# Moving one elementwise multiply of a gated attention layer from VectorE to GpSimd

## The chip, the core and the metric

The kernel runs on one NeuronCore of a Trainium2 chip. The core has five engines that run side by side, each through its own list of instructions, strictly in order: TensorE (PE) for matrix products, VectorE (DVE), ScalarE (ACT) and GpSimd (POOL) for elementwise work, and SyncE (SP), which here only starts memory transfers. An instruction that needs another engine's output waits for it, and everything behind it on its engine waits too. GpSimd in this kernel works on SBUF alone; PSUM, where TensorE writes, is read by VectorE and ScalarE.

The metric is the device time of one execution in microseconds, as a median over runs. It was 1340.9 us before the change (three runs, 1340.47 to 1341.65).

## The reference

One transformer layer on x of shape (4, 512, 512), all in fp32: a linear attention with 16 heads (key size 64, 64 memory slots, value size 128), a gate and a norm on its output, a layernorm, a mixture of 8 low-rank maps, and a second layernorm. What the change touches is the end of the attention:

```python
o = jnp.transpose(_chunk_abc(q, k, v, s), (0, 2, 1, 3))
g = (hidden_states @ Wg).reshape(b, t, H, DV)
o = o * jax.lax.rsqrt(jnp.mean(jnp.square(o), axis=-1, keepdims=True) + EPS) * g_norm_weight
o = o * (g * jax.nn.sigmoid(g))
return o.reshape(b, t, VALUE_DIM) @ Wo
```

The attention before it (okT is the query times hk) first sums keys into memory slots with a decay, takes a softmax over the slots, and then sums values with these weights:

```python
hk = hk * g_t[:, :, None, :] + k_t[..., None] * p_t[:, :, None, :]
pvT = jax.nn.softmax(okT, axis=-1)
hv = hv * g_t[..., None] + p_t[..., None] * v_t[:, :, None, :]
```

## The kernel before

The work is cut into 4 batch rows by 8 pairs of heads, 32 pairs in all, each over 512 time steps. Matrix products are made exact enough by splitting every fp32 operand into a rounded high part and the rest (names ending in h and l), and multiplying high by high, high by low and low by high. So nearly every value that TensorE reads is cast once (on ScalarE, mostly) and subtracted once (on VectorE or GpSimd). Weights are split once, kept in DRAM, and fetched again from there for every batch row by SP.

One pair goes through these kinds of step, each named by a letter:

- `s`, `k`, `q`, `g`, `v`: projections (decay, key, query, two gates, value), 12 matmuls of 512 columns each (value: of 256).
- `e`, `u`, `i`, `t`: transposes and states carried from one half of the time steps to the other.
- `c`: key scores (tiles `pa`), which ScalarE casts to `at`, VectorE subtracts and adds, and GpSimd cuts to the causal half (`causal`, an affine select). `x`: sums over them into `po_k`, which become `okc` (ScalarE copy `tk`, VectorE add), multiplied by `rc` on GpSimd.
- `o` (`soft`): the softmax, on VectorE, ScalarE and GpSimd. It turns `okc` over, takes maxima `mx`, subtracts (`pr`, GpSimd), exponentiates, sums `ss`, multiplies (`pr`, GpSimd), turns back, and ends in `wst`, the weights that TensorE needs next.
- `d`: value scores from `wst` and `est`; `y`: their sums into `po_v`. From `po_v` come the squares `sq`, their split `sqs`, and `t`, the output times its gate.
- `n` (`norm`, lines 972 to 1001): see below, twice for each pair, once for each head. `w` (`combine`): the output projection into `po_y`, four blocks of six matmuls that read `oh` and `ol`; VectorE adds each block to `y`.
- Letters `l`, `m`, `h`, `r`, `j`, `p`: loading and transposing x, and the second half of the layer for each batch row (`m`, `h` for the first three rows, `r`, `j` for the last). `b` and `f` start weight transfers on SP's queue, the first time and again.

The function `norm` is one matmul (`pt_ms`, the mean of squares over 128 channels) and five instructions after it, each on the engine that its `@on` names: "a" ScalarE, "d" VectorE, "p" GpSimd, "s" SP. First the logarithm and the exponential with factor -0.5 make the reciprocal norm `rstd` on ScalarE. Then VectorE multiplies `t` by it in place. Then ScalarE casts the product to `oh`, and GpSimd subtracts to get `ol`.

The order of the work is written out ahead of time, by a generator, in the string `PLAN` (lines 83 to 193). A letter alone issues the next step of that kind, that is its matmuls or its transfer. A mark and a letter issue the next instruction that a step of that kind still has for one engine: `^` ScalarE, `.` VectorE, `,` GpSimd, `;` SP; a number between them skips so many of them. So the string fixes the order on all five engines at once. Four more strings, `SLOTS`, say which of the 7 weight buffers (`wt`), 6 raw weight buffers (`wraw`), 7 work buffers (`tmp`, where `t`, `rstd`, `sq`, `cum`, `sg`, `okc` and others live) and 4 PSUM banks (`pa`) each new tile takes. A tile may be written when the one before it in its buffer has been read for the last time.

All instructions are recorded through one helper, so the profile shows line 56 for nearly all; tiles are told apart by their names.

Of the kernel before, what the change touches and what calls it, by code (L numbers as in the profile page):

```python
# [18 lines left out]
def tile_abc_attention_ffn(  # L19
# [22 lines left out]
    class InOrder:  # L42
# [41 lines left out]
        lpoooooooommoooooooooooooooooooooooorrrr,p,pbbbblbbl^l.ll^l.ll^l,b.l^l,b.ls,b;bb,1b^b,b.b^bq,b;bb.s  # L84
        ;1b.b^sb,b;bb.sek^q;b,sb.q^s,b^see.s^ke,s;b^kb^e.suuk^u^b,b.k,1b.e,b.ui.b^1k^i^i,b;bb.i.i;bb^i,ic^c
        ^c.c.1c^c;b,b.cb^k.c.cu,c^cs.k^b;p,c.c,b.c.b,c;bxb.cxx^b.s;b,cxbx.bx^sxxx.s,se;bxgb^s,s^x^s.x.sxx^ge
        ug.s^x^g.x^u,x^g.u^b.ge^g.oq^b.b^g.o;b^gb.b^o.g;bb.o^q.pv,o^b.q.b^oev^e.o;bb.e^oi^v.ov^i,o.v^i.i.i.o
        ^it,i^t.ov^t.t^o.t.o^bd^v.b^b.v;b^db.b^dg^d.d;b^d.1db.d.d,d.d,d.1d.dy^g.d,d^b,dy^g.by^g;b^yyb.g^yv
        ^1y.y^y.y.1yc,y.1y^c^c.y,y^cv.c^c.1c.yv^v.c.c,c.c,c.1cnxv.c^n.c,c.v^n,cx^b.nxxx^vx.bxxx^nx.vx;bx^xg
        ,nb^x.x^b.x.b,x;bsb^b.o.b.o;bb^o.s^s.ov,o^b.b,s^oeeee;bv.o^eb,s^o.et^v.o^t,o.v^t^g.tk.t^g.o^g.s.o^s  # L90
        .g^o^s.od^k.s^k^b.s^d.k^dq.d^d^d.1d.d.d,d.d,d.1d.du.du,d^qy.b^u,dy^b.q;byb^y.u.b^yy;b.yi^ybs.y^y^i,y
        .1y^i.1y.y.iv.i^b.s^i.b,i^sc;b.s,sb^c^c.c^sk.1c,s^c.c^s.c.c^c,c.s,c.cv.s^k,c^k.c^b.kxe^bxex.c^vux.b
        ,cxexx.vx^x;bnxb.b^n,yxxxt.x^n;bb.y^xv^t.n^t.x^nuq.t^u,x.t.u,n.o.oew^q^o.qw^e.o.w,o.ew^o.w.og^o.w.o
        ,o.op^gwb.o^p^g.pv^o.w;p^g.o^b.gd^v.b^b.v^d;b^db.dg^d.1d^d.d^b.d,d.d,d.1d.d.d,di.b^gy,d^i^g.by;bb^i
        ^gy.i;b^y.iy.gb^i^y,ink^1y.y^y.y^n.1y,y^n.1y.yc^1k.n^c^n.c^ks.c,nl^c.k^c.c^c,c.1c.c.c,c.cp,c.sxvb^p
        .c^b.p,c^sl.b;p^b,st.s;b^lbx,sv^t^t.l^su.tx^vx.tnx.b^sx,ynx^n.vx;bexbv.y^n.s^x.nxxxv.s^n.x^x,n.xp^vu
        vb,x^p.v^u.p^bv.o^b;p^b.u.o^be.bq^v^o.b;bb.v^b;b.ob^b.b,ow.b;b^qb^oeg.q;bb.o.w^o.b^b.o;bewb.b^e,o.b
        ;b^bbg^n.o^g;bb.e^n^g.o.n^gw^o.w^g.gw^g.o^n.w^g.wd,n.g^d^d.d^d.1ds^d.d.d,d.d,d.1d.d.d,d.bi,d^iy.s^i
        ;bby.i^s.it^i.s,s^1yy^t^t.ty^s.t,i^yg,s^s.y^y.s^y.y.s,y.1yc^g.y^c^g.yk^c.c^g.1c^c.c^c.g,c.c.c,cx.1cp
        ^k.cx^kb.c,c^p.kuex^b,cx.pxx^bee.bx;px^xxx.bv^b;bb.x^b;b^b.bbxxn^b.bv;b,y^xb.b;b^nbg^n.y;bb^v.x.n,x  # L100
        .v^n.bq^g,n^g.o;bb^g.o.g^ow^q.o,o.qw.w^o.onu.we^ow^u.o^e.uv,o^n.w.e^nn.ov^1n.n^1n.op^v.nwb^o.v^p.o^n
        .p^n,n.wd;p^b^d.b,n^dk^d.d;b^d.1db^b.d.d,d^b.d^b,d.1d.di.d^1k,dy.b^i^i,dy.i;b.i^ib.by^y,i.by;b^ybs.y
        ;b^yb.y^y.1y,y.1y.y,yc.s^c.y^s.c^kg.s,s^c^c^c.k^s,s.c.c^s.1cq^g.s,c^g.c^g.s,c.c.cp,c^q.gepb^px.cebx
        ^px.q,cxx^bx.pxex^xnx.p;px^bxux.x^nt.b^xl^n.b;bgb^t.x^t;p^l.n,x^b;b.t.t^b.lb^b.bw^g.o^b;bb^g.bw.o^b
        ;bb^g.wu^on.bw.g^u;bb.o.w,ov.u.w^ov.b^b.o;bb.b^ow.b;b^vb.o^ng;b.v,ob^b.w^n,n.o^n.b^bs.o^g;bb.n^g.b^o
        ^n.o;bb^ge,nw.s^e.g^s.e^b.s.wd^d^d,s^s.d^d,s.1dg^s.d.d^d.s,d.d.s,d.di.d^g,dy.b^i^gy.d;b^i,d^g.iyb.i
        ^i.gy^y,i^yv^1y.y^y.y.1yc,y.1y^c^c.y,y^cq.c^c.1c.y.c.c,c.c,cp.1c^qv.cb^p.c,c.q^b,c.p^bxxx.bx^v;pexx
        ^bx.bxxe^xx.vxx;b^bl;b.xn^xbee.b^lbw.x^n;bb.l^e,xfk^n.w.n.o.el.o^kfg.b^k^o.k;bb^l.o,o.lv^o^b.o.bu^ou
        t;b^u.ovb^t.u^t,o^g.t.t^gi.ow^v.o^g.v^i^ow.g^i.o^nf.i,n^b.i.w^i.wd^d^d,i.d^d^d.1ds.d.d,d.d,d.1d.d.d
        ,d.b,dy^b.s;byb.b^st^1y;b.s,sy^t^ty.t^s.t,sk^y^s.y^y.s^y.y.s,y^1kf.1yc^c.y^c.y^kg^c.c^c.k.c.c,c.1c.c  # L110
        v.c^gf,c.c^g,c.ce,ce^gxxxn.gxx^nx,yxxex^x.yxn^nxx.xev^x.n^e.x^nqf.e^v,xf.v,n.o.on^qwf^o.qu.ov.w,o^ow
        .o^ow.w.ou,oq.w^u^n.u.o^2n^n.o^1n.n^ow.nf.o^nf.wd^nf,n^d^d.d,n^d.1dv^d.d.d,d.d,di.1d^vy.d^i.d,d^i.v
        ,dy.i.i^iy,i^y^yy.ys^y.y^y,y.1y.1y.y,yc^b.s^c.y^s.c^ck.s,s^q^c^c.q^s,s.c.c^s.1cg^k.s,c^k^b.c.s,c.c.c
        xt,c^gf.k^txe^g.cxx.b,cxv^t^g.t;b.t.bux.gx;bx^xxnx.xx^nexv^x^n.xef.ne^vv,xf^e.v.ew.o.ow.w^o.ouv.w,o
        ^u.u^og^v.o.v^o.o,ov^gf^g.oi^g.ow^i.g^i^o.i.iw.o^i,i.w^nf.wdf,n^d^d.d^d.1ds^d.d.d,d.d,d.1d.d.d,dy,d
        .sfy^st^1y.s,s^ty^t.tv^s.t,s^y^s.yy^b.sk^v.y^y.s^y,y.v^b.y.yc^1kf.y^c.b^c^k.cg;b^c.1c^c.k.c.c,c.c,c
        .1cv^gf.c.c,c^g.b,cx^gxux;bee.gnxx^nu,yxxxe^ux.y^nxxx.uv^x.n^x.x^ne.xg^v,n^e.v.e,xw.o^gf.o^gv^o.w^g
        .mw.g.o,oi.w^iq^i.m^o.i.o^m^m.m^o.mwf.i^q.o^i.q,om.wm^2m,i.og^2m.m.o^o.3m.ow^gf.3m^gf^g.wdf.g^d^d.m
        ^dv.d^d.d^m.d^m,dg^b.mf^v.m.d.d,d.1d.d.d,dm.v^gfy,d^m.bm^gy.m;b^mn^g.my^y.gy^yk^n.y^y.y^n,y^y.n.y^nf
        .yc^1k,n^c.y^c^ks^c.k^c.c.1c.c.c,c.cnqf,c.1cb.c,y.c.s,c.y,c^s.sxx,s^qexexxt.q^sx,sg^n^s^n.s^t.n^t^x  # L120
        .su^nxefx.th^g.t,n.x^g^g.gxx^hxw^h^b,hex.w^ev^x.b.e;bnhb.x^n,x^n.n.on^hw.o^hf^1n,hw.w^o^1n.nuv^u.w^b
        .o.u,ow.b^v^nfg.v^o;b,nb^n.w.o,n^oh.o^gf,o^g^g.o.gw^hf.o^hw^o.w^b.oi.bm^i^i.w;bw^m,h.i.i^i,i.wd^d^d
        .d^d.1dh^d.d.d,d.d,d.1d.d.d,dy,d^hfm^hy.m,hm^yy.m^yy.ym.y^yk^y.m,y.1y.y.ym^1k,yf.mc.y^c^c^k.cs^m.1c
        ^c.k^c.m.c.c,c.cnqf,c.1c.c.c,c.s,c^s.s,sxx^qxfmv.q^m^s,s.m^nxxv^s^n.s.nmf^vxfee.sx^mumx.v^xxh^1m.xxx
        .mufx^ut^x.ue^mh.x^t.m^t,x.t.t.ogf.m.o^m^o.m.om,of^om.m.om^o.m.ow.m,o^nf.oe^gvf,n^e.w^g.ov^g.e^o.gn
        ^vm.o^n.vf^n.mdf.n^d^d.d^n.1dh^d.d,n^d.d.d.1d,d.d.d,dm,dyf^m,dt.m^ti^my^t.m^iy^i^y.t.ty^y.i.i^ig.y^y
        ,i.y^y.1y,y.1y.y,yc^gf^g.y^c^gs.c^c.g^c.c^c.c,c.1c.cx.cm,cf.ch,c.s.c^s,c.s,sxxfxx^sexx,s^mxk^s.m^x.s
        ^m.x.sn.m^kxfxxv^k^n.k^nux.nee^xm.x,xn.mmm^1n.1m^1n.oeg^e.n.o.m^o.eu.omf^u,o.m.u^ow.2m^m^m.ov.m^o.m
        ;m.w;mmmmmf.o^vf.1m,o^gf.v^gwf.o^g.mg.o.g^o.w.ow.m^gf^gw^m.w^g^mf.g^nf^n.wd,n.m^d^d,n^dq.d^d;m.1d.d
        .d,d.d,d.1d.dy.d,d^qf.mi,d.q^iy;m^i.iy.i^y^iy^y,is^1y.y^y.y.1y,y.1yl.y,yc.s^c.y^s.cf^ck,s.s^c^c,s.c  # L130
        ^s.c.1c^svf.c,c^k.s^k,c.cv.s,c.cn.k^vxxex.c^nux.vx,cex^nxxxx^xx.next^x.x^te.xu^tq^e.t,x.t^u.e.u.o.ov
        ^qf^o.qi.o,o^iw^i.i.i^i^o,iw.w.ow^o.w.ow.w,o^nf.onvf,n^n.w^n.osf^v.nf^o.v^n.o,nd.sf^s^d.s,s^dg^d^d.d
        ^s.1d,s.d^s.d.d,d.sv^gf,d^g.d.sl,d^gy.d^l.gv.d.l,dy^vy.v^y^yy.yv^y.y^y,y.1yw.1y.y,y.wc.y^c^c.c^ck.1c
        ^c.c.c,c.c,c.1c.c.c,cxl^kf,cxx^kn^l.kxxux^nx.lxex^xxex^nx.xt^x.ne^ten^t.xq^e.t,x.t.e.o.ow^qf^o.quv.o
        ^u.w,o.ugf^of^v.o.v^o^1n.ow,o^gf^1n.o^gg.n^g.o.g^o.ww.o^gf^gf^n.wdf^n,n^g^d.gg,n^d.d^d^d.1d.d.d,d.d
        ,d.1dl.d^gf.dy,d^ll,d^g.li^ly^g.ly^i.g^i^yy.i^y.is^i.y^y,i.y^y.1y,y.1yw.yf,y.s.yv^s.w,s.s,sc^c^s.ck
        ^c.c^s,c.c^c.s^c.c.s,c.cev^kf.1c^k.c.c,c.kxx,c^vxxxen.vex^nnxxx^xv^n.x^1n.nx^1nxxt^x.n^tuu.xw^t^u.t
        ,x.t.uv.w.owf.o^vf^o.vw.w.o^nf,oeq.w^nf,n^e^o.e.o,n^ogf^q.o,o.q.ow^gf.o^gv^o.w^g.o.gd^d^d.d^d.1ds^d
        .d.d,d.d,d.1d.d.d,dy,d.sfv^s.s,si^vy^i.v^sy,s^i^s.iy.i^i.s^yk,i^y.s^1y.y^y.y.1y,yc^1kf.1y.y^c,y^c.c
        ^kq.1c^c.y^c.k.c.c,c.c,cv.1c^qf.c.c,c.qx,cxnxx^nxexxx^nuxx^xxe.neut^u.x^tx.ug^t^x.t.t.x,xw^gf.o^g.ow  # L140
        ^g.w^o.gv.o.w,osf^of^v.o.v^o.owf,o^nf.ovf,n.w.oev^e.s^o.e^sg.o^v.s.v^s^sdf^g.s^d.s^g,s.dg^d^g.d,s.d
        ^d.g^d,d.d.d,d.1di^gf.dv.d^i,d^g,d^i^g.iy.i^i.gy,iy^y^yy.yv^y.y^y,y.1yfc^vf.1y^c.y^c.v^ck^c.c.1c.c.c
        ,c.c,c.1cn.c^kvf.c,c^k^n,y.kn,c^n.yexxx^1nxux.nx^1nv^x.n^n.xxe^v,nt^t.vxex^tx.txx.tg^x.x,xuw.o^gf^u
        .o^g.uw^o.w^g.mv.g.o.w,ov.m^owf^m.of^v^m.v^onq.m^1n.m.o^1n.w,o.m.om^qfem^2m.og^e.n^o.q^2m.o.3mw.e^gf
        .3m^gf^n.wdf^n,n.m^g^d.gs,n^m^d.d^m.1d^d^d.m.m.d.d,dv.df,d.1d.d.dv,d.s,d^si.s,st^i^i^ty.i^t.i^s.ty,s
        .t^i^sy^y.s,iy^y.sk^v.y^y.v^y.y.1y,yc.1y^1kf.y^c,y^c.c^kv.1c^c.y^c.kv.c.c,c.c,c.1cqf^vf.c.c,c.v,cxu
        ^qufxnm^u.q^nxx.um^mxx^n.mnxx^mex.nx^xexx.meg^x.x^1n.x^1n,x.nh^gf.o^g.o^g^o.gw^1hf.o,oeh.w^o^e.o.e^o
# [47 lines left out]
    def f(t):  # L195
# [8 lines left out]
            04152041520415364201543620136541362054120536  # L204
        """,
        "wraw": """
            0123450132450132450132450132450132450132450132450132450132450132450132450132450132450132514032514032
            5140325140325140325140404032
        """,
        "tmp": """  # L210
# [1175 lines left out]
```

## Time and profile before

| | |
|---|---|
| median of 3 runs | 1340.9 us |
| the profiled execution | 1339.01 us |
| its span, first to last instruction | 1337.3 us |
| granted TensorE clock | 0.998 |
| instructions | 24043 |
| bytes moved by DMA | 212.36 MB, mean 159 GB/s |

The profile comes from one execution. Busy times are those of the intervals in which an engine had an instruction at work. PE is matmuls and PEld the loading of their stationary operand, which overlap. In rows of the form "line engine operation out<-in shapes xcount | busy us, mean ns | idle before us", the last part is the time that the engine stood idle just before these instructions, and who ended it. In the table of stretches, each engine has its busy microseconds and, in brackets, its number of instructions, and the last three columns are the granted clock, the busy share of the 16 DMA engines, and GB/s. In rows of waits, the three numbers are microseconds in total, times, and the longest. In rows of the timeline, the first two numbers are start and duration in microseconds, and square brackets hold the idle time before and its releaser.

### The profile page before, as it was taken

What the parts mean: (1) busy time and instruction counts of PE and PEld (TensorE: products, weight loads), DVE (VectorE), ACT (ScalarE), POOL (GpSimd) and SP (SyncE); (2) the same over time, 40 slices, a digit from 0 to 9 for tenths busy, and PEclk for the clock granted to TensorE, in tenths of its full rate; (3) what the DMA queues carried; (4) which work ended last, traced back from release to release, by engine and by line L of the source; (5) the groups of instructions that cost most, each with busy time, mean ns of one, the idle gap of its engine ahead of it and who ended that gap; (6) DMA issues with size and microseconds to landing.
All of it is one profiled execution on the core that took longest, in us unless ns stands there. A gap on an engine that the chain in (4) does not pass through costs nothing.

```text
span 1337.3 us, 24043 instructions
## 1 busy us (share of the span) xinstructions
PE 1317.9 (99%) x8706; PEld 1139.0 (85%) x8706; DVE 1084.5 (81%) x2075; ACT 847.2 (63%) x1858; POOL 553.5 (41%) x623
## 2 busy tenths in 40 slices
PE   9999999999999999999999999999999999999997
PEld 7878888888888888888888888888888888888885
DVE  5888999988788778877779678878778887877855
ACT  4767787766676556666566655666666666666632
POOL 8344444444434343534343533334433344453310
PEclk9999999999999999999999999999999999999999
DMA  9555767763444346433344433544444343344452
GB/s 323 181 166 174 260 197 243 251 209 119 156 143 151 127 142 205 162 130 135 98 146 139 170 111 126 188 143 135 150 142 136 101 158 127 117 136 142 143 173 95
DMA packets 94007, 212.36 MB, mean 159 GB/s; under 512 B 12992, under 2 KB 43712, under 8 KB 93888
## 3 DMA queue, kind: packets, MB, share of 16 engines
q1 hardware_dynamic: 93360, 210.56, 46.9%
q8 instruction: 69, 1.13, 0.3%
q14 instruction: 50, 0.41, 0.1%
q10 hardware_dynamic: 528, 0.26, 0.1%
HBM read 162.55 MB, written 48.23 MB: 158 GB/s over the span
## 4 chain that ended last, share of the span: by engine, by line
PE 87%; DVE 7%; ACT 3%; POOL 1%; issue 1%; DMA 0%; SPq 0%; POOLq 0%; ACTq 0%; DVEq 0%
PE po_y L56 12%; PE ps_g L56 12%; PE ps_v L56 12%; PE po_v L56 7%; PE ps_s L56 6%; PE ps_k L56 6%; PE ps_q L56 6%; PE pa L56 5%; PE po_k L56 4%; PE ps_h L56 3%; PE po_f L56 3%; PE ps_vx L56 3%; PE pt_s L56 3%; PE pt_ms L56 1%; DVE at L56 1%
## 5 line engine op out<-in xcount | busy, mean ns | idle before, releaser
L56 POOL TENSOR_SCALAR_AFFINE_SELECT at<-at 128x512 fp32r<-128x512 f32 x256 | 170.8, 689 | 137.2 <-DVE at L56 123.3
L56 PE MATMUL po_y<-wt,oh 128*128 128x512 f32 x512 | 176.2, 396 | 0.1
L56 DVE TENSOR_TENSOR at<-pa,at 128x384 fp32r<-128x384 f32 x256 | 131.5, 549 | 7.4 <-ACT at L56 6.7
L56 POOL TENSOR_TENSOR ol<-t,oh 128x512 fp32r<-128x512 f32 x64 | 85.7, 1347 | 113.4 <-ACT oh L56 112.9
L56 ACT CAST at<-pa 128x384 fp32r<-128x384 f32 x256 | 107.5, 492 | 29.9 <-PE pa L56 28.2
L56 PEld LDWEIGHTS po_y<-wt,oh 128*128 128x128 f32 x512 | 96.3, 188 | 20.2 <-DVE okc L56 0.3
L56 PE MATMUL po_y<-wt,ol 128*128 128x512 f32 x256 | 100.2, 391 | 0.2 <-POOL ol L56 0.2
L56 DVE TENSOR_TENSOR y<-y,po_y 128x512 f32<-128x512 f32 x128 | 86.8, 680 | 11.6 <-PE po_y L56 10.7
L56 POOL TENSOR_SCALAR sqs<-sq 64x512 fp32r<-64x512 f32 x64 | 50.0, 781 | 95.1 <-DVE sq L56 84.0
L56 PE MATMUL po_v<-at,vh 128*128 128x256 f32 (+1 forms) x512 | 87.4, 278 | 0.0
L56 POOL TENSOR_TENSOR okc<-okc,rc 128x512 f32<-128x512 f32 x32 | 43.8, 1370 | 98.6 <-DVE okc L56 98.6
L56 PE MATMUL po_k<-at,ee 128*128 128x256 f32 (+3 forms) x512 | 82.9, 287 | 0.9 <-POOL at L56 0.8
L56 ACT ACTIVATE sq<-po_v 64x512 f32<-64x512 f32 x128 | 75.1, 591 | 9.5 <-PE po_v L56 7.5
L56 PEld LDWEIGHTS po_v<-at,vh 128*128 128x128 f32 x512 | 77.9, 190 | 0.9
L56 ACT ACTIVATE sg<-ps_g 128x512 f32<-128x512 f32 x64 | 38.2, 597 | 60.7 <-PE ps_g L56 55.7
L56 PEld LDWEIGHTS po_k<-at,ee 128*128 128x128 f32 (+1 forms) x512 | 69.0, 163 | 5.8 <-POOL at L56 2.1
L56 POOL TENSOR_TENSOR pr<-pr,mx 128x512 f32<-128x512 f32 x32 | 34.0, 1062 | 90.3 <-DVE mx L56 89.9
L56 POOL TENSOR_TENSOR pr<-pr,ss 128x512 f32<-128x512 f32 x32 | 33.9, 1059 | 88.5 <-DVE ss L56 62.4
L56 PE MATMUL po_v<-at,vl 128*128 128x256 f32 (+1 forms) x256 | 69.9, 273 | 0.3 <-POOL at L56 0.3
L56 DVE TENSOR_TENSOR at<-at,pa 128x128 fp32r<-128x128 f32 x256 | 62.8, 279 | 0.4
L56 DVE TENSOR_TENSOR t<-po_v,gate 128x512 f32<-128x512 f32 x64 | 44.1, 689 | 20.9 <-ACT sq L56 18.0
L56 POOL TENSOR_SCALAR est<-et 128x512 fp32r<-128x512 f32 x32 | 39.0, 1218 | 52.3 <-PE pa L56 23.7
(303 smaller groups left out, 3873.5 us busy)
## 6 DMA issues: line engine op xcount, KB each, us to landing
wt<-kept_v SPq DMA_DIRECT2D x48, 512.0 KB, 3.7
wt<-kept_g SPq DMA_DIRECT2D x48, 512.0 KB, 3.4
wt<-kept_o SPq DMA_DIRECT2D x48, 512.0 KB, 3.7
wt<-kept_s SPq DMA_DIRECT2D x24, 512.0 KB, 4.0
wt<-kept_k SPq DMA_DIRECT2D x24, 512.0 KB, 3.8
wt<-kept_q SPq DMA_DIRECT2D x24, 512.0 KB, 3.7
kept_g<-wt SPq DMA_DIRECT2D x16, 512.0 KB, 5.5
kept_v<-wt SPq DMA_DIRECT2D x16, 512.0 KB, 4.1
```

The costliest lines, as they stand in the source:

```text
L56: ins = fn(*args, **kwargs)
```

## The change

In `norm`, the multiply of `t` by `rstd` is issued to GpSimd in place of VectorE. Everything else that is computed, and with which instruction on which engine, stays. `PLAN` and the four strings of `SLOTS` were generated again for the kernel with this instruction on GpSimd, so the order of steps and the turns of the buffers differ in most lines.

```diff
-        @on("d")
-        def _():
-            DVE.tensor_mul(t1, t1, j.pop("rstd"))
+        @on("p")
+        def _():
+            POOL.tensor_mul(t1, t1, j.pop("rstd"))
```

The beginning of `PLAN`, where the projections of query and key change places, and its end:

```diff
-        lpoooooooommoooooooooooooooooooooooorrrr,p,pbbbblbbl^l.ll^l.ll^l,b.l^l,b.ls,b;bb,1b^b,b.b^bq,b;bb.s
-        ;1b.b^sb,b;bb.sek^q;b,sb.q^s,b^see.s^ke,s;b^kb^e.suuk^u^b,b.k,1b.e,b.ui.b^1k^i^i,b;bb.i.i;bb^i,ic^c
...
+        lpoooooooommoooooooooooooooooooooooorrrr,p,pbbbblbbl^l.ll^l.ll^l,b.l^l,b.ls,b;bb,1b^b,b.b^bk,b;bb.s
+        ;1b.b^sb,b;bb.s^k;b,s^kbuue.ke^ueq^s,b.u^s.s,s;bb.sek^q,b^e.q^b,1b.e,b.bi^1k^i,b;b^ib.i.i;bb^i,ic^c
...
-        .m^yy.yh.y^y^y,y.1y.1y.y,ywf.m.y^mnw.w^n.m^nn.nw^1n.w^nfm^n.wf,n.nm.m^n,nm.mw.mw.w.rw.w^r^r.rw.r.wfh
...
+        .mfy^my^y.m^yy.yh.y^y^y,y.1y.1y.y,ywf.m.y^mnw.w^n.m^nn.ww,n^1n^nfm^n.wf,nm,n.m^nm,n.mw.mw.w.rw.w^r^r
```

The buffers' turns begin to differ in the same way, for the weights (`wt`) for instance:

```diff
-            0123456013245061324506245013415034156203415062341503462150346210534104162041530416256302564162543016
...
+            0123456012345601234560345612415624150362415603241562410536241056324564510645326451031260314510342651
```

## The prediction

> **What bounds the kernel now.** I read the page first: busy time by engine, then the chain that ended last.
>
> ```profile
> PE 1317.9 (99%) x8706; PEld 1139.0 (85%) x8706; DVE 1084.5 (81%) x2075; ACT 847.2 (63%) x1858; POOL 553.5 (41%) x623
> ...
> PE 87%; DVE 7%; ACT 3%; POOL 1%; issue 1%; DMA 0%; SPq 0%; POOLq 0%; ACTq 0%; DVEq 0%
> ```
>
> TensorE (PE) is busy for all but 19 us of the span. Next I asked for the busy time in five stretches, to see where those 19 us lie.
>
> ```profile
> 0.00:50.00 50.00, 45.72 (x264) 38.62 (x266) 34.79 (x60) 29.50 (x63) 32.13 (x44) 1.00 0.88 290
> 50.00:100.00 50.00, 47.02 (x347) 40.95 (x344) 42.79 (x84) 33.47 (x73) 21.92 (x25) 1.00 0.48 158
> 100.00:300.00 200.00, 198.79 (x1361) 172.42 (x1360) 184.59 (x346) 151.91 (x327) 90.41 (x97) 1.00 0.66 221
> 300.00:1300.00 1000.00, 998.41 (x6620) 865.15 (x6619) 801.76 (x1545) 623.16 (x1374) 407.78 (x458) 1.00 0.42 142
> 1300.00:1337.30 37.30, 27.99 (x125) 21.86 (x123) 20.60 (x43) 9.15 (x22) 1.29 (x1) 0.92 0.31 109
> ```
>
> The first column pair after the stretch is PE. It idles 4.3 us in the first 50, 3.0 in the next, 1.2 in the next 200, 1.6 in the thousand after, 9.3 in the last 37. The changed multiply runs from 64.7 to 1267.3 us, so of all idle time only 3.0 + 1.2 + 1.6 = 5.8 us lies beside it. VectorE (DVE) is 92% busy from 100 to 300 us and 80% after. Matmuls overlap (twelve of 512 columns take 2.72 us, 0.227 each, though one is shown as 0.39), so a wait under about 0.16 us stays hidden. The waits of PE name who was late:
>
> ```profile
> PE pt_k L56 <- DVE at L56: 0.9, 1, 0.9
> PE ps_k L56 <- DVE vl L56: 0.9, 1, 0.9
> ...
> PE ps_v L56 <- DVE et L56: 0.8, 1, 0.8
> ...
> PE po_y L56 <- POOL ol L56: 0.2, 1, 0.2
> ```
>
> DVE is named for most of it, about 5 us without the tail; the chain that the change touches ends in `po_y<-ol` and is named once, for 0.2 us. A memory transfer is named once, for 0.3 us at the start, so the weights are never late.
>
> **The change, part by part.** (1) *Removed from DVE.* The rows by shape of the multiply, of the subtraction that follows it on GpSimd (POOL), and of a POOL multiply:
>
> ```profile
> L56 POOL TENSOR_TENSOR ol<-t,oh 128x512 fp32r<-128x512 f32 x64 | 85.7, 1347 | 113.4 <-ACT oh L56 112.9
> ...
> L56 DVE TENSOR_TENSOR t<-t,rstd 128x512 f32<-128x512 f32 x64 | 47.9, 753 | 8.9 <-ACT rstd L56 8.1
> ...
> L56 POOL TENSOR_TENSOR okc<-okc,rc 128x512 f32<-128x512 f32 x32 | 43.8, 1370 | 98.6 <-DVE okc L56 98.6
> ```
>
> 47.9 us of DVE work go, with 8.1 us in which the in-order DVE stood waiting for `rstd`.
>
> (2) *Added to POOL.* The same operation, type and shape already runs there: `okc<-okc,rc`, an fp32 multiply in place, 1370 ns on average. I take that: 64 x 1.37 = 87.7 us, so POOL goes to 641 us, 48%. The bounds per instruction are the shortest and longest `okc`, 1283 and 1797 ns.
>
> (3) *DVE and POOL hold each other up.* The view by tile shows it:
>
> ```profile
> L56 DVE TENSOR_TENSOR t<-t,rstd x64: 648/692/1796, 64.7 to 1267.3; 128x512 f32<-128x512 f32 x64
> ```
>
> Minimum, median and maximum: one multiply took 1104 ns more than the median. Over 64 the excess is (753 - 692) x 64 = 3.9 us, which leaves DVE with the multiply. Laying the excess of every DVE instruction over its group's usual length beside the POOL instruction that ran meanwhile, the 64 `ol` account for 4.2 us and the 32 `okc` for 2.2, or 0.07 each. So the 64 new instructions put 64 x 0.07 = 4.4 us on DVE: 1084.5 - 47.9 + 4.4 = 1041 us, 78%. The Trainium skill speaks against the change here: "SBUF — State Buffer", section "SBUF: two separate sides", says that VectorE instructions with two SBUF inputs and GpSimd instructions share one port pair as an exclusive lock, where the loser blocks for the whole instruction. If each of the 64 blocked such a VectorE instruction for its full length, the estimate by that rule would be 64 x 1.3 = 83 us, DVE near 1120 us and still under PE's 1318. The rows show about a twentieth of that.
>
> What (1) to (3) are worth on the path: DVE causes about 5 us of PE's waits outside the tail and gets 4% lighter overall. Bounds: 0 (each wait has a single late instruction, and none is this multiply) and -5.8 us (all PE idle time there goes). I take -1.5, nearer to 0, because a 4% lighter queue shifts a late instruction by part of a microsecond.
>
> (4) *The norm's own path gets longer.* Matmul `pt_ms`, logarithm, exponential, multiply, cast `oh`, subtraction `ol`, then `po_y`. The multiply costs 1370 - 753 = 0.62 us more. From the timeline I took, for all 64, the time from the end of `ol` to the first matmul that reads it: 35 have over 10 us, 12 under 1.7, the tightest 0.1, 0.2, 0.5, 0.7, 0.9, 0.9. In most tight ones the cast starts long after the multiply (behind other ACT work, or for its buffer), which absorbs the 0.62. The last pair has no such cover, and its order is nearly kept:
>
> ```profile
> 1264.82 0.39 PE L56 MATMUL pt_ms<-sqs,meanw 128*128 128x512 f32 x1
> ...
> 1267.28 1.43 DVE L56 TENSOR_TENSOR t<-t,rstd 128x512 f32<-128x512 f32 x1
> ...
> 1268.80 0.62 ACT L56 CAST oh<-t 128x512 fp32r<-128x512 f32 x1 [1.55 <-DVE t L56]
> ...
> 1269.56 1.29 POOL L56 TENSOR_TENSOR ol<-t,oh 128x512 fp32r<-128x512 f32 x1 [1.40 <-ACT oh L56]
> ...
> 1271.78 0.39 PE L56 MATMUL po_y<-wt,ol 128*128 128x512 f32 x1
> ```
>
> The new order puts multiply, subtraction, multiply, subtraction on POOL. From the first exponential's end at 1265.3: multiply to 1266.7, cast to 1267.4, subtraction to 1268.7, second multiply to 1270.1, cast to 1270.8, `ol` to 1272.2, against its reader at 1271.78: 0.4 us late. Elsewhere the new order gives more room (median PE work from `pt_ms` to the first `po_y` 26.8 us, before 23.8, counting each step with its matmuls' time). In sum +0.5; bounds 0 and +12.9 (each `ol` late by the 0.62 and by one more POOL instruction of 1.35 us ahead of it, less its room).
>
> (5) *What queues behind the multiply.* POOL works in order, so the wait for `rstd` moves onto its queue. In the new order the multiply is followed by `ol` 32 times, by `okc` 14 times, by another multiply 7, by a softmax step `pr` 6; the causal selects that PE waits for after each score step have a multiply between scores and select in 1 of 64 cases. So the exposed place is the softmax, `okc` to `wst`:
>
> ```profile
> 1130.39 1.29 POOL L56 TENSOR_TENSOR okc<-okc,rc 128x512 f32<-128x512 f32 x1 [2.14 <-DVE okc L56]
> ...
> 1134.39 1.05 POOL L56 TENSOR_TENSOR pr<-pr,mx 128x512 f32<-128x512 f32 x1
> ...
> 1138.62 1.05 POOL L56 TENSOR_TENSOR pr<-pr,ss 128x512 f32<-128x512 f32 x1 [3.18 <-DVE ss L56]
> ...
> 1142.19 0.69 DVE L56 TENSOR_TENSOR wst<-w,wst 128x512 fp32r<-128x512 f32 x1
> ...
> 1142.90 1.33 PE L56 MATMUL pa<-wst,est 64*128 64x256 f32 x18
> ```
>
> PE starts 0.02 us after `wst` ends; in about half of the 32 pairs the room is under 0.1 us, so there a delay is paid in full. Today 18 of these POOL steps stand directly behind an `ol` or `hl`, and 2 were held up by it, by about 1 us. The 20 new neighbours at that rate: 20 x 2/18 x 1.0 us x one half = +1.1. Bounds: 0, and 20 x 1.35 x one half = +13.5. In the orders, the other POOL work inside this stretch rises from 0.8 to 1.5 us per pair while other DVE instructions fall from 14.1 to 13.0 (about 0.7 us each), and the PE work beside it stays 16.1 us: a balance, hence the small value.
>
> (6) *The rest of the new order.* PE keeps its 1513 steps, of which 79% stay in sequence; the 344 weight fetches and 101 stores on SP's queue keep 99% of theirs, except that key's first weights are now fetched and used before query's (transfers of 5.7 and 4.6 us to landing, covered by the matmuls of decay, the projection before). In the first 30 us PE waited 0.79 us for `kf`, 1.10 for a PSUM buffer at 26.08 and 0.28 for a select: 2.2 us. In the new order the key transposes stand straight behind key's matmuls: cast 0.58, copy 0.38 and about 0.3 until they start and land, 1.3 us late; and the third select is due at 28.2 (score steps to 25.1, decay 2.72, three sums of 0.12) but started at 28.49 and took 0.9: 1.2 late. That is 2.5: net +0.3, bounds -2.2 and +2.5. `t` and `rstd` hold two of seven work buffers longer; what would be late next is the writer that takes them (`cum`, `sg`, `tk`). I cost that at nothing: PE's order leaves those steps 10 us and more, and without that cover each would cost what `cum` or `sg` takes, about 1 us.
>
> Sum: -1.5 + 0.5 + 1.1 + 0.3 = +0.4 us. The profiled execution took 1339.0 us (span 1337.3 and 1.7 around it), 1.9 below the median of 1340.9. So 1339.4 for it, and 1341.3 as a median. The rivals count from 1340.9.
>
> **The rivals.** *A, faster:* the lighter DVE removes most of PE's idle time from 50 to 300 us (4.2 us), where DVE is busiest: about -4, 1336.9. For it: DVE is named in those waits. Against: these 200 us hold only a quarter of the multiplies. *B, slower:* the multiplies ahead of `okc` and `pr` are late, because ACT delivers `rstd` late, and hold the softmax up. Two full hits (2.7 us) decide; I price five, 5 x 1.35 = +6.8, 1347.7. For it: half the pairs have no room. Against: 2 of 18 today. *C, slower:* the second passage through POOL makes `ol` late in the tight pairs; half of the 12.9 is +6.4, 1347.3. For it: 12 pairs under 1.7 us. Against: the new order leaves more room.
>
> **How the numbers follow.** Forecast 0.46, A 0.24, B 0.22, C 0.08. About 0.2%, 2.7 us, is what a measurement of this kernel can tell from no change. Of the forecast 0.41 lies within it, 0.02 is faster, 0.03 slower; A gives 0.22 faster, 0.02 same; B 0.20 slower, 0.02 same; C 0.07 slower, 0.01 same. Faster 0.24, same 0.46, slower 0.30. The range runs from all of PE's idle time gone (-5.8) to a little above B and C (+7): 1335 to 1348, with about 0.17 outside. The forecast's own range is 1338.2 to 1343.6.
>
> **What would show it.** DVE near 1041 us, POOL near 641, the new row `t<-t,rstd` on POOL near 1370 ns, PE's busy time within 3 us of 1318. Right on (5): `okc` and `pr` on POOL wait for DVE as now. Wrong, and B: PE's waits name `wst`, and `okc` starts right behind a multiply. Wrong, and C: `po_y` waits for `ol`. Wrong, and A: PE idles under 2 us from 50 to 1300.

## The result

The changed kernel takes 1343.84 us (median of 9 runs, 1342.78 to 1344.24), the kernel before 1340.47 us beside it (9 runs, 1338.07 to 1341.65). The ratio is 1.0028, 95% interval 1.0019 to 1.0037: slower by about 3.8 us. The time lies inside the range that was given, 2.5 us above the predicted number and just above the forecast's own range (1338.2 to 1343.6); counted by the 0.2% that the prediction takes as the least that can be told, the outcome is "slower", to which 0.30 had been given (0.46 to "same").

The page of the changed kernel: span, busy time by engine, and the chain that ended last by engine. The profiled execution took 1343.96 us.

```profile
span 1342.2 us, 24000 instructions
...
PE 1319.6 (98%) x8706; PEld 1140.4 (85%) x8706; DVE 1055.7 (79%) x2011; ACT 847.6 (63%) x1858; POOL 638.9 (48%) x687
...
PE 83%; DVE 7%; ACT 4%; POOL 3%; issue 1%; DMA 0%; SPq 0%; POOLq 0%; ACTq 0%; DVEq 0%
```

The span grew by 4.9 us. VectorE (DVE) lost 28.8 us of work and GpSimd (POOL) gained 85.4, but TensorE (PE), which bounds the kernel, has the same 8706 matmuls to do, and its busy time grew by 1.7. In the chain, POOL went from 1% to 3%. The table of stretches of the changed kernel, the same five but for the last one's end, shows where PE stands still:

```profile
0.00:50.00 50.00, 44.80 (x254) 38.09 (x256) 34.67 (x59) 28.80 (x62) 31.67 (x44) 1.00 0.89 290
50.00:100.00 50.00, 46.52 (x349) 40.67 (x350) 41.74 (x82) 34.02 (x74) 22.14 (x25) 1.00 0.48 156
100.00:300.00 200.00, 197.31 (x1354) 171.80 (x1354) 181.69 (x334) 151.08 (x326) 104.26 (x107) 1.00 0.64 219
300.00:1300.00 1000.00, 996.93 (x6605) 863.43 (x6604) 773.89 (x1491) 622.28 (x1371) 478.19 (x511) 1.00 0.42 141
1300.00:1342.20 42.20, 34.07 (x152) 26.43 (x150) 23.73 (x50) 11.38 (x27) 2.59 (x2) 0.96 0.32 112
```

PE idles 5.2, 3.5, 2.7, 3.1 and 8.1 us, against 4.3, 3.0, 1.2, 1.6 and 9.3 before. So beside the multiply, from 50 to 1300 us, it idles 9.2 us instead of 5.8. The 1.2 us less in the last stretch is no gain of the change: in the profiled execution before, 4.3 us passed from the end of VectorE's last instruction to the end of the span, in this one 3.2, and 3.2 too in the other profiles of the order of before. Nothing big stands out; the loss is many small waits. These are the waits of PE in the changed kernel, those on the path in question:

```profile
PE po_k L56 <- POOL at L56: 2.0, 5, 0.8
PE po_v L56 <- POOL at L56: 1.6, 5, 0.6
...
PE po_y L56 <- POOL ol L56: 1.4, 2, 0.8
...
PE pa L56 <- DVE wst L56: 0.8, 3, 0.3
```

The kernel before had, for `po_k` and `po_v`:

```profile
PE po_k L56 <- POOL at L56: 0.8, 2, 0.6
...
PE po_v L56 <- POOL at L56: 0.3, 2, 0.2
```

Waits for POOL rose from 1.3 us (with 0.2 for `po_y`) to 5.0. `at` is the causal select of the scores, `ol` the end of the norm. The waits by all engines show how the change reaches them. First two rows of the changed kernel:

```profile
POOL t L56 <- ACT rstd L56: 44.2, 31, 3.2
...
ACT oh L56 <- POOL t L56: 13.2, 21, 2.1
```

and the row that stood in the place of the second in the kernel before:

```profile
ACT oh L56 <- DVE t L56: 6.2, 9, 1.5
```

POOL stands waiting for `rstd` 31 times, which is the wait that moved onto its queue. And ScalarE (ACT), which is in order too, now waits 21 times for the product before it can cast it, 13.2 us in all, against 9 times and 6.2 us. Each such wait also holds what is queued on ACT behind the cast.

### The profile page after: what moved, and what is told of

Same layout as the page of the kernel before. It is cut to its first block, busy times and chain, and to the rows that moved or that the text cites. A ratio compares the mean times of both kernels' runs of the same rounds, so it can differ in the third digit from the quotient of the medians.

```text
span 1342.2 us, 24000 instructions
## 1 busy us (share of the span) xinstructions
PE 1319.6 (98%) x8706; PEld 1140.4 (85%) x8706; DVE 1055.7 (79%) x2011; ACT 847.6 (63%) x1858; POOL 638.9 (48%) x687
## 4 chain that ended last, share of the span: by engine, by line
PE 83%; DVE 7%; ACT 4%; POOL 3%; issue 1%; DMA 0%; SPq 0%; POOLq 0%; ACTq 0%; DVEq 0%
PE ps_v L56 12%; PE ps_g L56 12%; PE po_y L56 11%; PE po_v L56 6%; PE ps_q L56 6%; PE ps_s L56 5%; PE pa L56 5%; PE ps_k L56 5%; PE po_k L56 4%; PE ps_h L56 3%; PE ps_vx L56 3%; PE po_f L56 3%; PE pt_s L56 3%; PE pt_ms L56 1%; DVE at L56 1%
## 5 line engine op out<-in xcount | busy, mean ns | idle before, releaser
L56 POOL TENSOR_TENSOR t<-t,rstd 128x512 f32<-128x512 f32 x64 | 85.9, 1346 | 46.7 <-ACT rstd L56 44.2
L56 POOL TENSOR_TENSOR okc<-okc,rc 128x512 f32<-128x512 f32 x32 | 42.9, 1340 | 58.2 <-DVE okc L56 58.1
L56 DVE SCALAR_TENSOR_TENSOR gate<-ps_g,gw_t,sg 128x512 f32<-128x512 f32 x64 | 47.7, 745 | 22.5 <-ACT sg L56 22.1
```

The lines of the kernel that those rows point to most:

```text
L56: ins = fn(*args, **kwargs)
```

## The experiments

All kernels below were timed in five rounds beside the kernel before; a ratio of 0.001 is 1.34 us. Four of them leave the product by `rstd` out of the output (the two without a multiply, and the two with memsets); the others that compute something else say so in their expectation.

### The order and the engine, each by itself

Four kernels take the two orders apart from the engine of the multiply. In the first, the order of the kernel before is kept with its turns of buffers, and the mark of the multiply in `PLAN` becomes GpSimd's, at the same place; in the second, the changed kernel's order is kept and the mark becomes VectorE's. In the other two the instruction and its mark are left out.

```diff
-        @on("d")
+        @on("p")
         def _():
-            DVE.tensor_mul(t1, t1, j.pop("rstd"))
+            POOL.tensor_mul(t1, t1, j.pop("rstd"))
```

> The order and buffer turns of before, with the multiply issued to GpSimd at the very place where VectorE had it. If the cost comes from the multiply being on GpSimd (queue behind it, or the lock between the two engines), an order not made for it pays at least what the change paid: +3 to +10 us over before, 1343.5 to 1350.5, and PE's waits name POOL (at, ol). If the cost lies in the new order alone, this kernel stays within 1.5 us of before, 1339 to 1342.

> The order and buffer turns of the change, with the multiply issued to VectorE at the same place. If the new order alone costs the time, it stays near the changed kernel, 1343 to 1345. If the multiply on GpSimd costs it, this falls back to 1340 to 1341.5. A mixture shows in between; the first 73 us, where the trace lags 1.1 us before more than two multiplies have run, should keep their loss in either case.

```diff
-        @on("d")
-        def _():
-            DVE.tensor_mul(t1, t1, j.pop("rstd"))
```

> The order of before with the multiply left out (the reciprocal norm is computed and not applied). It measures alone what 47.9 us less of VectorE work are worth on the path: the prediction said -1.5 us with bounds 0 and -5.8. If VectorE's load is what makes PE wait, -3 to -5 us, 1335.5 to 1337.5; if each wait has a late instruction of its own, -0.5 to -1.5, 1339 to 1340.

> The order of the change with the multiply left out. Against the changed kernel it shows all that the GpSimd multiply costs in this order, queue and lock together; against the old order without the multiply it shows what the order alone costs. If the multiply on GpSimd is the cause, 1339 to 1340.5; if the order is, 1342 to 1344.

Measured, as ratios to the kernel before with their intervals:

| the multiply | order of before | order of the changed kernel |
|---|---|---|
| left out | 0.9977 (0.9968 to 0.9986) | 0.9978 (0.9969 to 0.9987) |
| on VectorE | 1 | 1.0045 (1.0033 to 1.0058) |
| on GpSimd | 1.0088 (1.0074 to 1.0102) | 1.0028 (1.0019 to 1.0037) |

Three of the four came out otherwise than expected. The multiply on GpSimd in the order of before costs 11.6 us, where 3 to 10 were expected. The new order without the multiply is at 1336.1 us, under the 1339 to 1340.5 that were expected if the multiply on GpSimd is the cause. And the multiply on VectorE in the new order is at 1344.9 us, where it was expected if the order alone cost the time; the first row of the table shows that the order alone doesn't.

The first row answers the question about the order: without the multiply the two orders take the same time, so the new order by itself neither costs nor brings anything that can be measured. Each order is made for its own engine: a multiply on VectorE costs 0.23% (3.1 us) in its own order and 0.67% in the other; on GpSimd 0.50% (6.7 us) in its own, and 1.11% (14.9 us) in the other. The change is worth the difference of the two costs in their own orders, 6.7 - 3.1 = 3.6 us. Taking the multiply off VectorE is worth 3.1 us, its work there and its step in the norm's path together; on GpSimd it then costs more than twice as much.

### A load without reading, and a second multiply

To see what of the multiply costs on GpSimd, three memsets took its place: on `rstd`, on `t`, and on half of `t`. They hold POOL about as long, wait for the same, and the cast waits for them as for the product, but they read nothing.

```diff
-            POOL.tensor_mul(t1, t1, j.pop("rstd"))
+            POOL.memset(j.pop("rstd"), 1.0)
+            POOL.memset(t1, 1.0)
+            POOL.memset(t1[:, 0:256], 1.0)
```

> The changed kernel with the GpSimd multiply replaced by three memsets on GpSimd (over rstd, over t, and over half of t), so the product is not computed. They wait for the same things, are waited for by the same cast, and keep GpSimd about as long (512 + 512 + 256 columns; a memset of 512 took 0.52 us, so about 1.3), but read nothing from SBUF. If the multiply's cost is that it holds up VectorE instructions that read two SBUF tensors, the lengthening of w<-w,rc and wst<-w,wst (866 and 820 ns on average in the changed kernel) goes and the time falls to 1337 to 1340. If the cost is the time it takes in the path and in GpSimd's queue, the time stays at 1341.5 to 1344.5.

Measured: 1.0017 (1.0008 to 1.0025), between no multiply (0.9978) and the changed kernel (1.0028). The rows of the memsets in its lines by shape:

```profile
L56 POOL MEMSET t<- 128x512 f32 x64 | 33.8, 528 | 0.0
...
L56 POOL MEMSET rstd<- 128x512 f32 x64 | 33.7, 527 | 46.3 <-ACT rstd L56 46.0
...
L56 POOL MEMSET t<- 128x256 f32 x64 | 20.0, 313 | 3.7
```

They take 528 + 527 + 313 = 1368 ns, against 1346 for the multiply. The time, 1341.28 us, is just under the 1341.5 to 1344.5 that were expected if path and queue are the cost, and above the 1337 to 1340 of the other theory. So most of the cost (1.0017 - 0.9978 = 0.39% of 0.50%) remains when nothing is read.

The second edit issues the multiply twice, so that the norm is applied twice.

```diff
+            POOL.tensor_mul(t1, t1, j["rstd"])
             POOL.tensor_mul(t1, t1, j.pop("rstd"))
```

> The changed kernel with the multiply done twice on GpSimd (the norm is applied twice). The first multiply cost 0.50% (1336.06 to 1343.8, each against before). If its cost grows with the time in path and queue, the second costs at least as much, since the room left is smaller: 1350 to 1360. If the planned places have room, under +3 us.

Measured: 1.044 (1.0417 to 1.0462), 1397.9 us, 58.6 over the kernel before and far over the 1350 to 1360 that were expected. The first multiply costs 6.7 us in 64 instructions, 0.1 us each; the second some 55 us, 0.86 each. The waits of this kernel:

```profile
ACT oh L56 <- POOL t L56: 54.3, 31, 3.5
...
PE po_k L56 <- POOL at L56: 5.5, 8, 2.1
...
PE po_y L56 <- POOL ol L56: 4.0, 5, 1.2
```

ACT's wait for the product went from 13.2 to 54.3 us. Not all of this is waits: in the profiled execution (1403.07 us, 59 over that of the changed kernel) the granted clock was 0.984 instead of 0.999 and PE's busy time 1345.5 us instead of 1319.6, so 26 us lie in PE's busy time and 33 in its idle time (55.8 against 22.6). So the order has little room left for a second multiply, but its price holds the lower clock too.

### The product unused, and no wait for rstd

Here the product goes over `rstd`, which nobody reads afterwards, and the cast takes `t` as it is. The multiply stays in POOL's queue, waits for `rstd` and reads two operands, but no later step needs it.

```diff
-            POOL.tensor_mul(t1, t1, j.pop("rstd"))
+            POOL.tensor_mul(j["rstd"], t1, j["rstd"])
```

> The changed kernel with the product written over rstd, where nobody waits for it: the cast and the subtraction take t without the norm. GpSimd's work, its wait for rstd and its hold on VectorE stay; the path from norm to output projection no longer has the multiply in it. If the longer path is the cost, the time falls to 1337 to 1338.5. If the queue behind the multiply and the lock are the cost, 1341 to 1344.

Measured: 1.0005 (0.9996 to 1.0014), 0.23% below the changed kernel, 1339.4 us, which lies between the two expectations. The 0.23% (3.1 us) are the part of the path.

In the next, `t` is multiplied by itself, so POOL doesn't wait for `rstd`.

```diff
-            POOL.tensor_mul(t1, t1, j.pop("rstd"))
+            POOL.tensor_mul(t1, t1, t1)
```

> The changed kernel with t multiplied by itself on GpSimd in place of by rstd, so GpSimd does not wait for ScalarE there (44.2 us in the changed kernel) and the cast does not either. Work and hold on VectorE stay. If the wait at the head of GpSimd's queue makes the causal selects and okc late, PE's waits on POOL at (3.6 us in the changed kernel) go and the time falls to 1338 to 1340; if not, 1342 to 1344.

Measured: 1.0003 (0.9995 to 1.0012). Its waits and its row:

```profile
ACT oh L56 <- POOL t L56: 3.0, 4, 1.9
```

```profile
L56 POOL TENSOR_TENSOR t<-t 128x512 f32<-128x512 f32 x64 | 68.1, 1069 | 0.0
```

This run doesn't separate what it was meant to. Without the wait the product is there before the cast's turn, so the norm's path went as well (ACT's wait for `t` fell to 3.0 us), and with one operand in both places the instruction takes 1069 ns instead of 1346. It agrees with the run before in size, no more. One thing it adds: VectorE was lengthened more here than in the changed kernel (1063.4 us busy against 1055.7), and the time is lower all the same.

### The path alone, the queue alone

Three memsets again, but all on `rstd`. The cast no longer waits for them. What is left is POOL's time and its wait.

```diff
-            POOL.tensor_mul(t1, t1, j.pop("rstd"))
+            rstd = j.pop("rstd")
+            POOL.memset(rstd, 1.0)
+            POOL.memset(rstd, 1.0)
+            POOL.memset(rstd[:, 0:256], 1.0)
```

> The changed kernel's order with three memsets, all onto rstd, in the multiply's place: the cast doesn't read them, so the norm's path has no step on GpSimd before ol; they read nothing in SBUF, so VectorE isn't lengthened. What stays is the wait for rstd on GpSimd's queue and about 1.37 us of its time. The product is left out. The version with memsets on t was at 1.0017, the one without a multiply at 0.9978. If the queue itself costs (behind it stand selects, okc, pr and ol): 0.999 to 1.001. If the path was all of it: 0.997 to 0.9985.

The changed kernel was run again beside it:

> The changed kernel as it is, beside the two below on the same chip. Its ratio to the kernel before was 1.0028; every theory expects 1.002 to 1.004 again.

Measured: the changed kernel 1.0031 (1.002 to 1.0042), as before; the memsets off the path 0.9989 (0.998 to 0.9997). That falls between the two expectations, so the queue costs something, and the path more. All in the order of the changed kernel:

| in the multiply's place | POOL's time and wait | cast waits | SBUF read | ratio |
|---|---|---|---|---|
| nothing | | | | 0.9978 |
| memsets on `rstd` | x | | | 0.9989 |
| memsets on `rstd` and `t` | x | x | | 1.0017 |
| the multiply, product unused | x | | x | 1.0005 |
| the multiply | x | x | x | 1.0028, 1.0031 |

Row by row: the queue 0.0011 (1.5 us), the path 0.0028 (3.8 us) where nothing is read and 0.0023 to 0.0026 (3.1 to 3.5 us) between the last two rows, the reads 0.0016 (2.1 us) where the product is unused and 0.0011 to 0.0014 where it is used. 1.5 + 3.8 + 2.1 = 7.4 us, where the multiply as a whole costs 6.7 to 7.1. Each ratio is uncertain by about 0.0009, so the shares are uncertain by about 0.0012 (1.7 us): the path is clear of zero by that, the reads and the queue are at its edge.

Two spots show how this comes about. The first shows the reads and the end of the norm; the timeline of the changed kernel, a pair in the first batch row:

```profile
239.61 1.29 POOL L56 TENSOR_TENSOR t<-t,rstd 128x512 f32<-128x512 f32 x1 [0.66 <-ACT rstd L56]
239.66 1.79 DVE L56 TENSOR_TENSOR wt<-wraw,wt 128x512 fp32r<-128x512 f32 x1
...
240.94 0.62 ACT L56 CAST oh<-t 128x512 fp32r<-128x512 f32 x1 [0.37 <-POOL t L56]
...
241.38 0.68 DVE L56 TENSOR_TENSOR wst<-w,wst 128x512 fp32r<-128x512 f32 x1
...
241.64 1.55 POOL L56 TENSOR_TENSOR ol<-t,oh 128x512 fp32r<-128x512 f32 x1 [0.73 <-ACT oh L56]
...
243.24 0.50 PE L56 MATMUL po_y<-wt,ol 128*128 128x512 f32 x1 [0.84 <-POOL ol L56]
```

and the same steps in the kernel with the memsets off the path, where PE doesn't stand:

```profile
237.75 1.48 POOL L56 MEMSET rstd<- 128x512 f32 x3 [0.63 <-ACT rstd L56]
...
237.82 0.68 DVE L56 TENSOR_TENSOR wt<-wraw,wt 128x512 fp32r<-128x512 f32 x1
...
238.75 0.69 DVE L56 TENSOR_TENSOR wst<-w,wst 128x512 fp32r<-128x512 f32 x1 [0.26 <-ACT wst L56]
...
239.32 1.29 POOL L56 TENSOR_TENSOR ol<-t,oh 128x512 fp32r<-128x512 f32 x1
...
240.73 0.44 PE L56 MATMUL po_y<-wt,ol 128*128 128x512 f32 x1
```

DVE's `wt<-wraw,wt` starts 0.05 us after the multiply and takes 1.79 us instead of 0.68, so `wst` behind it starts 1.77 us after the multiply's start, against 1.00 after the memsets'. And `ol` starts 2.03 us after it, against 1.57, and takes 1.55 us instead of 1.29, which here is too late for PE. For that wait the path is enough: with the memsets also on `t`, which read nothing, PE stands nearly as long at this place:

```profile
241.62 0.50 PE L56 MATMUL po_y<-wt,ol 128*128 128x512 f32 x1 [0.72 <-POOL ol L56]
```

The two waits of PE for `ol` in the changed kernel, here and at the last pair (0.84 and 0.52 us), come back in its second profile (1.12 and 0.50) and with the memsets also on `t` (0.72 and 0.54); with the product unused and with the memsets off the path there is none, and without any multiply there is one, of 0.26 us at the first place.

The second spot shows ACT's queue. The timeline of the changed kernel in the last batch row:

```profile
1155.86 1.29 POOL L56 TENSOR_TENSOR t<-t,rstd 128x512 f32<-128x512 f32 x1
...
1157.18 0.62 ACT L56 CAST oh<-t 128x512 fp32r<-128x512 f32 x1 [1.09 <-POOL t L56]
...
1157.83 1.20 ACT L56 ACTIVATE sq<-po_v 64x512 f32<-64x512 f32 x2
...
1160.76 0.69 DVE L56 TENSOR_TENSOR t<-po_v,gate 128x512 f32<-128x512 f32 x1 [0.42 <-ACT sq L56]
...
1161.51 0.24 PEld L56 LDWEIGHTS po_k<-qst,s 64*128 64x128 f32 x3 [0.28 <-DVE t L56]
```

and with the memsets off the path:

```profile
1151.00 1.48 POOL L56 MEMSET rstd<- 128x512 f32 x3
...
1151.16 0.61 ACT L56 CAST oh<-t 128x512 fp32r<-128x512 f32 x1
...
1151.94 1.20 ACT L56 ACTIVATE sq<-po_v 64x512 f32<-64x512 f32 x2 [0.17 <-PE po_v L56]
...
1154.90 0.69 DVE L56 TENSOR_TENSOR t<-po_v,gate 128x512 f32<-128x512 f32 x1 [0.32 <-ACT sq L56]
...
1156.21 0.25 PEld L56 LDWEIGHTS po_k<-qst,s 64*128 64x128 f32 x4
```

The cast waits 1.09 us for the product. Behind it on ACT stand the squares of `po_v` of the next pair's two heads, then DVE's products with the gate, which read the same `po_v`, and only when the second is read can PE go on: it stops for 0.28 us amid the four loads of `po_k`. Nothing of this belongs to the norm that was delayed; its own `ol` has time here.

Matched step by step on PE, whose order is the same in both, the kernel with the memsets also on `t` falls 3.3 us behind the one with the memsets off the path: 2.0 at three places of `po_y` (the end of the norm), 1.4 at three places of `po_k`, and the other steps cancel but for 0.1. (Among them are 0.5 at one `ps_v`, before which PE waits 1.3 us for `et`, as in the changed kernel, and 0.8 with the memsets off the path, and -0.4 before the first memset, which the edit can't have made.) So in this pair of traces the path's cost is the end of the norm for the larger part; that the rest is what stands behind the cast fits, but was followed at one place. Only the two spots shown were traced back to their cause.

### Norms whose cast is late anyway, and the others

Back in the order of before, the 64 norms were split by one criterion: whether the cast to `oh` started at least 1.3 us after the multiply's end in the trace of before. 31 do; there the longer multiply has cover. One kernel has these 31 multiplies on GpSimd, the next has the other 33.

```diff
+        far = 2 * (u["b"] * NPAIR + u["p"]) + h in FAR
-        @on("d")
+        @on("p" if far else "d")
         def _():
-            DVE.tensor_mul(t1, t1, j.pop("rstd"))
+            (POOL if far else DVE).tensor_mul(t1, t1, j.pop("rstd"))
```

> The order and the buffers of the kernel before. The multiply is on GpSimd for the 31 norms of 64 whose cast to oh started at least 1.3 us after the multiply had ended in the trace of before (ScalarE was behind anyway), and on VectorE for the other 33. With all 64 on GpSimd in this order the time rose by 11.6 us. If the longer path through the norm were what costs, these 31 have cover and the time stays within 1.5 us of before (ratio 0.999 to 1.001). If the occupied GpSimd queue and the longer VectorE instructions are what costs, they pay their share, 31/64 of 11.6: +4 to +6 us (1.003 to 1.0045).

> The complement of the run with the 31 far norms: in the order of the kernel before, the multiply is on GpSimd for the 33 norms whose cast started less than 1.3 us after the multiply in the trace of before, and on VectorE for the 31 others. If the cost is the longer path through the norm, nearly all of the 11.6 us that 64 multiplies cost in this order returns: +9 to +13 us (ratio 1.0067 to 1.0097), with ScalarE's cast named as waiting for GpSimd's t about as long as with all 64 (15.9 us). If the cost were the number of multiplies on GpSimd's queue, growing faster than their number, half of them cost less than half: 0 to +5 us (1.000 to 1.0037).

Measured: the far 31 at 0.9995 (0.9986 to 1.0004), the near 33 at 1.0056 (1.0042 to 1.007), and all 64 had been at 1.0088. So half of the multiplies move for nothing and the other half bring 7.5 us. The waits of ACT name the difference; the kernel with the far 31:

```profile
ACT oh L56 <- DVE t L56: 7.0, 11, 1.5
```

and the one with the near 33, as many as with all 64 in this order (15.9 us, 25 times):

```profile
ACT oh L56 <- POOL t L56: 15.9, 25, 2.1
```

The theory of the path alone had asked for +9 to +13 us from the near ones; 7.5 is short of that, and well over the 5 us that the theory of numbers alone would allow. The two halves add up to 6.8 us where all together cost 11.6 to 11.8, so about 5 us come only when both halves are on POOL. The split isn't pure either: beside the far multiplies 10 DVE instructions were lengthened by 6.9 us in all, beside the near ones 21 by 17.0 us. The far version is level with the kernel before; no version here beats both kernels by more than the measurement can tell.

## Why the prediction was right or wrong

The sum was +0.4 us, measured was about +3.8. The time lies in the stated range because that range was drawn to hold the rivals B and C as well; the forecast's own range ended at 1343.6. Term by term:

**(1) What DVE's relief is worth.** Predicted -1.5 for (1) to (3) together (bounds 0 and -5.8); leaving the multiply out gives -3.1 us. The sign and the bounds held. But the -3.1 holds more than the relief: the multiply's step in the norm's path goes with it, and the 6.2 us for which ACT's cast waited for it. No run takes away one without the other. Nor do the traces show where the -3.1 lies: of the 3.0 us between the two profiled spans, 0.9 come before the first multiply, 1.0 between the first and the last, and 1.2 after PE's last matmul. So the size rests on the medians, and the way to it stays open. The busy time that goes is smaller than the 47.9 us of the row: without the multiply, DVE is at 1043.0 us in the new order and 1045.6 in the old, 41.5 and 38.9 less, partly because neighbours on DVE overlap by 0.07 to 0.09 us.

**(2) The cost on POOL.** 1370 ns predicted from `okc`, 1346 measured; POOL 641 predicted, 638.9 measured. Right:

```profile
L56 POOL TENSOR_TENSOR t<-t,rstd 128x512 f32<-128x512 f32 x64 | 85.9, 1346 | 46.7 <-ACT rstd L56 44.2 <-PE pt_s L56 2.3
```

**(3) DVE and POOL hold each other up.** This term was mis-sized. The prediction averaged the lengthening beside the old POOL instructions, 0.07 us each, and put 4.4 us on DVE. From the kernel without a multiply to the changed one it is 1055.7 - 1043.0 = 12.7 us, 0.20 each, so DVE is at 1055.7 us where 1041 were forecast. The tiles show whom it strikes. In the changed kernel (count, shortest/median/longest in ns):

```profile
L56 DVE TENSOR_TENSOR w<-w,rc x32: 660/693/1821, 47.7 to 1254.6; 128x512 f32<-128x512 f32 x32
```

```profile
L56 DVE TENSOR_TENSOR okc<-po_k,tk x64: 671/683/686, 33.7 to 1243.1; 64x512 f32<-64x512 f32 x64
```

and in the kernel with memsets on `rstd` and `t`:

```profile
L56 DVE TENSOR_TENSOR w<-w,rc x32: 658/691/1008, 46.6 to 1251.2; 128x512 f32<-128x512 f32 x32
```

`w<-w,rc` reads two operands from SBUF and took up to 1821 ns beside the multiply; before it was 956 at most, beside memsets 1008. `okc<-po_k,tk` reads one from PSUM and was never longer than 686 ns, though 19 of its 64 ran beside a multiply. Laying all DVE instructions over the multiplies in the trace: 39 with two SBUF operands ran beside one, 31 of them were lengthened, by 18.0 us in all, `w<-w,rc` by up to 1.1 us; of the 99 others none by more than 31 ns. So the rule that the prediction set aside is right in its conditions: the Trainium skill, "SBUF — State Buffer", section "SBUF: two separate sides", names a VectorE instruction with two SBUF inputs against a GpSimd instruction that reads SBUF, and the trace shows just these two conditions, the second by the memsets. What was wrong was to turn it into a cost by an average (0.07 each) or by one full hit per multiply (83 us): what counts is how many such VectorE instructions the order puts beside it, here 39 for 64. In time, the reads cost 1.5 to 2.1 us, so (1) to (3) together are -1.0 to -1.6, where -1.5 had been predicted: two errors that nearly cancel, which is luck.

**(4) The norm's own path.** This is the step that failed. Predicted +0.5 us (bounds 0 and +12.9), measured +3.8 with memsets and +3.1 to +3.5 by the product unused. The measured figures are for the whole step on GpSimd, the predicted one for what it costs more there than on VectorE. Matched step by step on PE in the profiled executions, at the steps of `po_y`, where the norm ends, the multiply on VectorE in its own order costs 0.1 us against none, on GpSimd in its own 1.9, so there most of the difference stands. The working laid the room between `ol` and `po_y` over a table of the old order and found cover: "In most tight ones the cast starts long after the multiply (behind other ACT work, or for its buffer), which absorbs the 0.62." For the new order it took that there is more room on average, and checked a single pair. The room didn't grow where it was tight: in the changed kernel 12 of the 64 `ol` end less than 1.7 us before their first reader and 35 over 10 us, just as before. Two things were missing. First, single pairs of the new order without that cover: at 243 us PE stands 0.84 us for `ol`, where nothing was predicted. Second, who stands behind the cast: it waits for the product 21 times and 13.2 us, and ACT's queue waits with it, as the second spot shows. The split fits this: the norms whose cast has cover cost nothing, those without it 7.5 us, though part of that is the reads. For the last pair the prediction was near: `ol` was to be 0.4 us late, and PE stands for 0.5:

```profile
1277.75 0.50 PE L56 MATMUL po_y<-wt,ol 128*128 128x512 f32 x1 [0.52 <-POOL ol L56]
```

**(5) What queues behind the multiply.** Predicted +1.1, measured +1.5 with the memsets off the path: right within the uncertainty. The place was not quite the one named: with these memsets PE's waits for `wst` from DVE went from 0.5 to 0.8 us, and its waits for the selects before `po_k` and `po_v` from 2.1 to 3.0 (1.5 and 0.6 in this order without any multiply). The prediction had called the selects safe because a multiply stands ahead of them in 1 of 64 cases. The other 1.0 us of waits for selects, from 1.1 to 2.1, belongs to the new order and is made good elsewhere in it. The sign that was given, that `okc` on POOL waits for DVE as now, was not met: it waits 58.1 us, 98.6 before the change.

**(6) The rest of the order.** Predicted +0.3, measured 0.0: without the multiply the two orders are equal within 0.0013. The trace shows the loss at the head: in the first 50 us, before any multiply, PE idles 0.9 us more than before. Where it is made good shows between the two kernels without a multiply: PE's busy time is 1.2 us less in the new order (1315.6 against 1316.8).

The sum of the measured terms, -3.1 + 2.1 + 3.8 + 1.5 + 0 = +4.3 us, stands to +3.6 to +4.2 for the whole (ratios 1.0028 and 1.0031), within what the shares are uncertain by.

**The rivals.** A (faster, 1336.9) is out: PE idles more from 50 to 1300 us, and the place where it looked for the gain holds none. With the multiply left out in the order of before, PE still idles 4.3 us from 50 to 300, against 4.2 with it:

```profile
50.00:100.00 50.00, 47.00 (x338) 41.08 (x339) 41.79 (x83) 33.45 (x74) 22.85 (x26) 1.00 0.48 157
100.00:300.00 200.00, 198.69 (x1354) 172.35 (x1354) 178.17 (x334) 150.86 (x326) 88.58 (x96) 1.00 0.65 222
```

B (slower through the softmax) is out as it was described, since PE waits for `wst` 1.3 us in all, against 1.0 before. C (slower through a late `ol`) is the nearest to what happened, at a third of its price: PE waits for `ol` 1.4 us at two places instead of 0.2 at one, and the steps at `po_y` cost 2.0 of the 6.4 us it was given. It was put at 0.08. The rest of the loss is spread over the longer path on ACT's queue, the reads and POOL's queue, with no rival of its own.

## What to carry to other kernels

When an instruction moves to a slower engine, look at the instruction that consumes it, and not only at the end of its path: if the consumer already waits for this product, everything behind it in its engine's queue becomes later; if it starts late for another reason, the move can be free, as it was for the 31 norms here. Count beforehand, in the order that will run, how many two-operand SBUF instructions of VectorE will stand beside each GpSimd instruction that reads SBUF; an average over the trace says little. And to price a move, leave the instruction out once in each order: that separates what the old place cost (3.1 us here) from what the new one costs (6.7).

## What the runs showed that was not expected

The cost of work on a partly idle engine is far from linear: POOL is at 48% of the span with the multiply and at 52% with a second one, yet the second costs some 55 us where the first costs 6.7, though some of the 55 goes with a granted clock of 0.984 instead of 0.999. A multiply with the same operand in both places took 1069 ns on POOL where two operands took 1346, and a memset of the same shape 528. And an order written for one engine is worth much to that engine alone: 0.60% for the multiply on GpSimd and 0.45% for the one on VectorE, while without the multiply the two orders differ by nothing that can be measured.
